# One of five convolution inputs is made by an accumulating DMA, and its siblings an iteration sooner

## The chip, the cores and the metric

The kernel runs on one core of a Trainium2 chip. The metric is the device time of one execution in microseconds; runs of one kernel lie within some tenths of a per cent of each other. A core has five engines that run side by side, each with its own queue of instructions: TensorE (PE in the profile, its weight loads PEld), VectorE (DVE), ScalarE (ACT), GpSimd (POOL) and SyncE (SP), which issues nearly all DMAs here. An instruction waits for semaphores of other engines at the head of its queue, and everything behind it in that queue waits too.

## The reference

Four modulated 1-D convolutions (64 channels, 3 taps, no activation between them) are run one after the other on each of 128 samples of 64 x 1024 floats, and the result is added to the input. Each sample has its own weights: the shared weight, scaled per input channel by a style vector and normalised per output channel.

```python
def _layer(x, style, w, b, mw, mb, typ):
    s = style @ mw.T + mb
    weight = SCALE * w * s[:, None, :, None]
    demod = lax.rsqrt(jnp.sum(weight * weight, axis=(2, 3)) + EPS)
    weight = weight * demod[:, :, None, None]
    if typ == 'same':         # layers 0 and 2
        out = conv_same(x, weight) + b
    elif typ == 'upsample':   # layer 1
        out = blur(conv_up(x, weight) + b, 2.0 * blur_k, (1, 1))
    elif typ == 'downsample': # layer 3
        out = conv_down(blur(x, blur_k, (2, 2)), weight) + b
    return out

out = x
for i, typ in enumerate(('same', 'upsample', 'same', 'downsample')):
    out = _layer(out, cond_512, weights[i], biases[i], mod_w[i], mod_b[i], typ)
return x + out
```

## The kernel before

**One convolution in place of four.** With nothing nonlinear between the layers, their chain is, away from the ends of a row, one convolution of nine taps whose weights differ from sample to sample. The kernel works out these nine taps for each sample on TensorE (stage1, stage2, stage3: small 64x64 matmuls), adds the residual as an identity in the middle tap, and applies them to the row. The ends of the rows are worked out apart, in a few extra slots of matmuls.

**Fewer products by sums and differences.** A row is stored as three planes (every third element), so that nine taps make three output planes out of three times three products. Instead of nine products per group, the kernel makes five: it forms five inputs T0 to T4 from sums and differences of the planes, five weight sets (three of them, H, by `combine_a` and `combine_b` on VectorE), multiplies them (`conv0` to `conv4`, each 24 records of 64x64 weights on 340 columns) and adds up the outputs (`sum1`, `sum2`, `output`).

**Tiling.** Four samples make a quad: two in the upper and two in the lower 64 partitions of two tiles, so that four 64x64 matmuls use the array at once. There are NQ = 32 quads. Each quad's input X holds 128 partitions x 2 x 3 planes of 344 floats (PL = 344).

**The inputs of a quad q.** X has two buffers, G one, each of T04, T12 and T3 two:

- `in_g2(q)` and `in_g01(q)` (VectorE, L768 and L763, both recorded at L712): G, three planes made out of X
- `in1(q)`: T1 = G plane 2 + G plane 1 (GpSimd, L776)
- `in2(q)`: T2 = G plane 2 - G plane 1 (GpSimd, L781)
- `in04(q)`: T0 and T4, differences of G's planes (VectorE, L790)
- `in3(q)`: T3 = a difference of X's planes (VectorE, L761)

**The order.** All instructions are written out by hand; no planner reorders them. The early turns (`early_turn`, quads 0 to 3) and the last three quads have orders of their own. The steady turn is `turn_of(q)`, for q = 4 to 28. With n = q+1, c = q+2 and s = q+4, a turn finishes quad q, does most of n, starts on the inputs and taps of c, and runs stage1 of s. On TensorE a steady turn is: stage2 of c (`stage2_rest`, L589 and L506), conv2(q), stage3_b(c), conv4(q), stage3_a(c), conv3(n), stage1_a(s), conv0(q), stage1_b(s), `share` (L506), an extra slot in turns 10, 14, 15 and 19 (L1044), conv1(n).

What the steps of the prediction touch, by engine:

- VectorE, in this order: sum2(q) (L712 into Y, then L862), combine_a(n) and combine_b(n) (L712 into H, L709), in04(n), share_sums (L501), in_g2(c), the side work of the turn (dictionary `SIDE`, work for the rows' ends and for constants, another one in each turn), stage1_b's sums (L481), in_g01(c), rest of an extra slot, sum1(n) (L712 into y), in3(c).
- GpSimd: r_sums(c) (L638, two of R's slots are sums), in2(n), now and then tables, stage1_b's addition (L484), in1(c).
- ScalarE: copies and scalings out of PSUM (L399), the outputs (L880), `share_copy` (L529). share_copy writes the PSUM banks that stage1_b's sums have read, and stage2_rest of the next quad adds onto what it wrote.
- SP: the loads of X (L146) and the stores of the outputs (L885).

Before a steady turn q starts, T1(n) has thus been made at the end of turn q-1, T2(n) follows in turn q behind R's sums, and T0/T4(n) in the middle of turn q on VectorE.

Of the kernel before, what the change touches and what calls it, by code (L numbers as in the profile page):

```python
# [48 lines left out]
F32 = mybir.dt.float32  # L49
AF = mybir.ActivationFunctionType  # L50
ALU = mybir.AluOpType
# [12 lines left out]
def kernel(  # L64
# [10 lines left out]
    NP, P, NXC = x.shape  # L75
    B = 2 * NP
    NQ = B // 4
# [5 lines left out]
    nc_v, nc_a, nc_g = nc.vector, nc.scalar, nc.gpsimd  # L83
# [3 lines left out]
    const = ctx.enter_context(tc.tile_pool(name="const", bufs=1))  # L87
# [4 lines left out]
    wf_pool = ctx.enter_context(tc.tile_pool(name="wf_pool", bufs=3))  # L92
    tpool = ctx.enter_context(tc.tile_pool(name="tpool", bufs=2))
    mpool = ctx.enter_context(tc.tile_pool(name="mpool", bufs=1))
    gpool = ctx.enter_context(tc.tile_pool(name="gpool", bufs=1))
    opool = ctx.enter_context(tc.tile_pool(name="opool", bufs=2))
    ps_conv = ctx.enter_context(tc.tile_pool(name="ps_conv", bufs=2, space=PSUM))
    ps_w = ctx.enter_context(tc.tile_pool(name="ps_w", bufs=1, space=PSUM))
# [39 lines left out]
    PL = NXC // 3  # L138
# [35 lines left out]
    NB = 340  # L174
# [222 lines left out]
    def scaled_copy(eng, dst, src, f):  # L397
        if eng is nc_a:
            nc_a.activation(dst, src, AF.Copy, scale=f)  # L399
        else:  # L400
            eng.tensor_scalar(dst, src, f, None, op0=ALU.mult)
# [158 lines left out]
    def stage2(q, pool=None, engs=(nc_a, nc_a), between=None):  # L560
        if q in shared_ps:
            ps = stage2_rest(q)
        else:
            ps = opened.pop(q, None)
            taps = range(9) if ps is None else range(3, 9)
            ps = stage2_taps(q, taps, ps or unit(pool or ps_w, f"psR{q}"))
        if between:
            between()
        t = r_pool.tile([P, 2, 9, C], F32, tag="R", name=f"R{q}")
        for r in range(2):  # L570
            scaled_copy(engs[r], flat(t[:, r, :7]), ps[r][:, : 7 * C], tC[:, q, r : r + 1])
        chain[q] = t
        return ps
# [3 lines left out]
    def stage2_taps(q, taps, ps):  # L577

        st = chain[q]
        for n in taps:  # L580
            e = n - 2
            if e % 2 == 0:
                a, lo, m = slice(1, 4), e // 2 + 1, 3
            else:
                a, lo, m = slice(4, 6), (e + 3) // 2, 2
            for r, rows in enumerate(HALF):
                for c, cols in enumerate(HALF):
                    src = st[c if r == 0 else 1 - c]
                    nc.tensor.matmul(  # L589
                        ps[r][cols, lo * C : (lo + m) * C],  # L590
                        E[rows, e + 2, :],
                        src[rows, a, :],
                        start=(n == 0),
                        stop=(n == 8),
                        skip_group_check=True,
                    )
        return ps
# [38 lines left out]
    def r_sums(q, eng):  # L636
        t = chain[q]
        eng.tensor_add(t[:, :, 7:9], t[:, :, 2:6:3], t[:, :, 3:7:3])  # L638
# [97 lines left out]
    Ts = {}  # L736
    Gs = {}
# [5 lines left out]
    def plane(buf, i, pairs=BOTH_PAIRS):  # L743

        at = PL * (2 - i) if i < 3 else PL * 2 + 1
        return buf[:, pairs, at : at + NJ]
# [16 lines left out]
    def in_g01(q, pairs=BOTH_PAIRS):  # L763
        if q < NQ:
            X, g = g_tile(q)
            sum_of(g[:, pairs, PL:], X[:, pairs, : 2 * PL], 0.5, X[:, pairs, PL:], ALU.subtract)

    def in_g2(q, pairs=BOTH_PAIRS):  # L768
        if q < NQ:
            X, g = g_tile(q)  # L770
            sum_of(plane(g, 2, pairs), plane(X, 3, pairs), 0.5, plane(X, 2, pairs), ALU.subtract)

    def in1(q, eng):
        if q < NQ:
            t, g = t_tile(q, "T12"), Gs[q]
            eng.tensor_add(t[:, :, 0, :NJ], plane(g, 2), plane(g, 1))  # L776

    def in2(q, eng):
        if q < NQ:
            t, g = t_tile(q, "T12"), Gs[q]  # L780
            eng.tensor_sub(t[:, :, 1, :NJ], plane(g, 2), plane(g, 1))  # L781

    def in04(q, pairs=BOTH_PAIRS):
        if q < NQ:
            t, g = t_tile(q, "T04"), Gs[q]
            a, b = g[:, pairs, :NJ], g[:, pairs, 2 * PL : 2 * PL + NJ]
            both = lambda v, step: bass.AP(
                v.tensor, v.offset, [*(list(d) for d in v.ap[:-1]), [step, 2], [1, NJ]]
            )
            nc_v.tensor_sub(t[:, pairs, :, :NJ], both(a, PL), both(b, 1))  # L790

    def product(q, m, ps, groups=range(K), alone=False):

        W, H_ = Wq[q]
        tag, i = SLOT[m]
        for g in groups:
            for s, rows in enumerate(HALF):
                for c, cols in enumerate(HALF):
                    if m in (0, 4):
                        w = W[rows, tap(m // 2, g), c, :]  # L800
                    else:
                        w = H_[rows, m - 1, g, c, :]
                    nc.tensor.matmul(  # L803
                        ps[s][cols, :NB],
                        w,
                        Ts[q, tag][rows, c, i, g : g + NB],
                        start=(g == 0 and (m == 3 or alone)),
                        stop=(g == K - 1),
                        skip_group_check=True,
                    )  # L810
# [36 lines left out]
    def sum1(q):  # L847

        y1w[q] = m_tile("y1", q, 2)
        for s, a in parts(q):  # L850
            sum_of(y1w[q][:, s], a, 2.0, m3c[q][:, s])
# [4 lines left out]
    def sum2(q, steps=(0, 1)):  # L856
        if 0 in steps:
            m3 = m3c.pop(q)
            for s, a in enumerate(banks(q)):
                sum_of(Y[:, s, :NB], m3[:, s], 3.0, a[:, :NB])  # L860
        for s, a in parts(q) if 1 in steps else ():
            nc_v.tensor_sub(y1w[q][:, s], y1w[q][:, s], a)  # L862
# [24 lines left out]
            os[q][:, s, planes].rearrange("c i j -> c (i j)"),  # L887
        )


    raw = const.tile([P, 512], F32, name="raw")

    WIDE = 6
    ends_ps = {}
# [94 lines left out]
    g1 = const.tile([P, 6, C], F32, name="g1")  # L989

    Ye = [const.tile([P, HB, 8], F32, name=f"Ye{s}") for s in range(2)]
    Ue = [const.tile([P, HB, 11], F32, name=f"Ue{s}") for s in range(2)]
    Ve = [const.tile([P, HB, 12], F32, name=f"Ve{s}") for s in range(2)]
    Oe = const.tile([P, B, 3], F32, name="Oe")
# [295 lines left out]
    def small(q):  # L1290
        l, bs = SMALL[q]
        dst = high(bs.stop - bs.start)
        src = c0f if l == 0 else cc[l - 1]
        for cols in HALF:
            nc.tensor.matmul(
                dst[cols], wsum[T, l, :], src[T, bs], start=False, stop=True, skip_group_check=True
            )
# [66 lines left out]
    def side(work, q):  # L1364
        work.get(q, lambda: None)()
# [117 lines left out]
    def turn_of(q):  # L1483
        n, c, s = q + 1, q + 2, q + 4
        entry = q == FIRST
        stage2(c)
        if entry:
            sum2(q)
            conv4(q)
            combine_a(n)  # L1490
            r_sums(c, nc_v)
        else:
            conv2(q)
            r_sums(c, nc_g)
            sum2(q)
            in2(n, nc_g)
        side(TABLES, q)
        for i in range(3):
            load(c + 1, slice(i, i + 1))
        stage3_b(c, open_a(n))  # L1500
        if entry:
            conv0(q, 0, 1)
        else:
            combine_a(n)
            conv4(q)
        stage3_a(c)
        combine_b(n)
        conv3(n)
        if entry:
            copy_m3(n)  # L1510
            stage1_a(s)
        outputs(q, 2)
        if not entry:
            if s < NQ:
                stage1_a(s)
            copy_m3(n)
        in04(n)
        if sharing(q):
            share_sums(c + 1)
        in_g2(c)  # L1520
        side(SIDE, q)
        if q in SMALL:
            l, bs = SMALL[q]
            nc_v.memset(high(bs.stop - bs.start), 0.0)
        conv0(q, *((2,) if entry else range(K)))
        if entry:
            conv1(n, 0, 1)
        outputs(q, 1)
        if s < NQ:
            stage1_b(s)  # L1530
        in_g01(c)
        if sharing(q):
            share(c + 1, banks(q))
            share_copy(c + 1)
        outputs(q, 0)
        if q in SLOTS:
            matmuls, width, rest = SLOTS[q]
            slot(matmuls, width, Y_banks)
            rest()
        if s == NQ:  # L1540
            slot(ends3, 3, unit(ps_w, "psE"), 3)
            rest3()
        conv1(n, *((2,) if entry else range(K)))
        if q in SMALL:
            small(q)
        sum1(n)
        in3(c)
        side(LATE, q)
        if s == NQ:
            in04(c)  # L1550
        in1(c, nc_g)
        if s + 1 < NQ:
            scale3(s + 1)

# [3 lines left out]
        turn_of(q)  # L1558

    q, n, c = NQ - 3, NQ - 2, NQ - 1  # L1560
    stage2(c)
    conv2(q)
    in2(n, nc_g)
    stage3(c, 0)
    sum2(q, (0,))
    combine_a(n)
# [26 lines left out]
    q, n = NQ - 2, NQ - 1  # L1593
# [128 lines left out]
```

## Time and profile before

| | |
|---|---|
| median of 3 runs | 475.84 us (475.61 to 476.85) |
| profiled execution, span | 475.5 us (first to last instruction; of this execution no other time is given) |
| TensorE busy / weight loads | 469.7 us / 349.5 us |
| VectorE, ScalarE, GpSimd busy | 417.3, 312.0 and 165.8 us |
| granted clock of TensorE | 0.998 |
| DMA | 70.71 MB, queue of SP 46.3% of 16 engines |

A line of the timeline reads: start, duration, engine, line, operation, output<-input with partitions x elements, count, and in brackets the idle time of the engine ahead of it with what ended it. Neighbouring instructions of one kind are merged (x2 and so on). Where a helper records many operations they all carry its line: L712 is `sum_of`, L399 `scaled_copy`. Lines of the page's fifth part give a group: its count, its busy time and the mean duration of one in ns. Matmuls overlap, so the pace of TensorE is read from the distance between starts.

### The profile page before, as it was taken

The page shows a single profiled execution, that of the slowest core. Times are in us where ns is not written, and L with a number is a line of the kernel's source. Part 1 is how long each engine was busy: PE and PEld are TensorE (multiplying, and loading weights), DVE is VectorE, ACT ScalarE, POOL GpSimd, SP SyncE. Part 2 cuts the span into 40 slices and gives each one's busy share as a digit, 9 for nine tenths or more (in the row PEclk, how much of TensorE's full clock was granted, in tenths as well). Part 3 has the DMA queues.
Part 4 walks back from the last instruction along what each step waited for, and adds up shares of the span by engine and source line. Part 5 has one row for each costly group of instructions (what it writes and reads, how often), then busy time and mean ns, then how long its engine had stood idle before and what let it go on. Part 6 is the DMA issues. An engine that isn't in the chain of part 4 may idle for free.

```text
span 475.5 us, 26771 instructions
## 1 busy us (share of the span) xinstructions
PE 469.7 (99%) x11932; PEld 349.5 (74%) x11932; DVE 417.3 (88%) x694; ACT 312.0 (66%) x711; POOL 165.8 (35%) x200
## 2 busy tenths in 40 slices
PE   9999999999999999999999999999999999999996
PEld 6987788777678876677776677766788787876653
DVE  3889998879989998899979899979998999999896
ACT  4565657577766676766667666667666777766464
POOL 3634033664444342233432233422333423243200
PEclk9999999999999999999999999999999999999999
DMA  5237456535445554345544454543555544455225
GB/s 176 71 115 224 150 151 180 152 113 177 139 145 166 166 166 136 123 150 169 163 150 126 130 168 152 178 124 121 152 164 169 164 145 147 148 152 161 80 91 193
DMA packets 52707, 70.71 MB, mean 149 GB/s; under 512 B 6000, under 2 KB 50672, under 8 KB 52592
## 3 DMA queue, kind: packets, MB, share of 16 engines
q1 hardware_dynamic: 52368, 68.78, 46.3%
q8 instruction: 93, 1.52, 1.4%
q10 hardware_dynamic: 224, 0.22, 0.1%
q14 instruction: 22, 0.18, 0.1%
HBM read 35.36 MB, written 33.62 MB: 145 GB/s over the span
## 4 chain that ended last, share of the span: by engine, by line
PE 99%; DVE 0%; ACT 0%; issue 0%
PE psA L803 47%; PE Y L803 12%; PE psR L506 9%; PE psW L621 7%; PE psA L621 7%; PE psS L428 6%; PE psR L589 5%; PE psA L506 2%; PE Y L1044 2%; PE Y L183 1%; PE Y L379 1%; PE psM L220 0%; PE psE L1044 0%; PE Y L255 0%; DVE o L882 0%; PE psM L255 0%
## 5 line engine op out<-in xcount | busy, mean ns | idle before, releaser
L803 PE MATMUL psA<-T,H 64*64 64x340 f32 x2304 | 185.9, 446 | 0.0
L803 PEld LDWEIGHTS psA<-T,H 64*64 64x64 f32 x2304 | 90.7, 133 | 46.9 <-issue 2.5
L712 DVE SCALAR_TENSOR_TENSOR G<-X 128x1376 f32<-128x1376 f32 (+2 forms) x65 | 78.0, 1206 | 0.2
L776 POOL TENSOR_TENSOR T<-G 128x684 f32<-128x684 f32 x28 | 46.3, 1652 | 73.7 <-DVE G L712 73.7
L484 POOL TENSOR_TENSOR S<-S 128x128 f32<-128x128 f32 x28 | 21.6, 772 | 139.7 <-ACT S L399 139.6
L399 ACT ACTIVATE R<-psR,tC 128x448 f32<-128x448 f32 x63 | 36.6, 631 | 43.6 <-PE psR L506 25.8
L803 PE MATMUL psA<-T,Wf 64*64 64x340 f32 x768 | 63.7, 446 | 0.0
L803 PE MATMUL Y<-T,Wf 64*64 64x340 f32 x768 | 62.4, 451 | 0.0
L712 DVE SCALAR_TENSOR_TENSOR Y<-m,psA 128x340 f32<-128x340 f32 x62 | 32.0, 516 | 28.2 <-PE psA L803 26.9
L399 ACT ACTIVATE psW<-psA 128x128 f32<-128x128 f32 x100 | 19.3, 268 | 49.1 <-PE psA L621 45.0
L790 DVE TENSOR_TENSOR T<-G 128x1368 f32<-128x1368 f32 (+1 forms) x33 | 50.8, 1541 | 0.0
L399 ACT ACTIVATE Wf<-psW,t 128x256 f32<-128x256 f32 (+2 forms) x76 | 32.7, 480 | 26.7 <-PE psW L621 26.4
L761 DVE TENSOR_TENSOR T<-X 128x684 f32<-128x684 f32 x32 | 47.7, 1492 | 0.0
L506 PE MATMUL psR<-S,E 64*64 64x64 f32 (+1 forms) x1472 | 46.8, 237 | 0.0
L781 POOL TENSOR_TENSOR T<-G 128x684 f32<-128x684 f32 x28 | 46.5, 1660 | 0.0
L428 PEld LDWEIGHTS psS<-wd,w2n 64*64 64x64 f32 x1120 | 35.1, 133 | 12.9 <-issue 0.3
L506 PEld LDWEIGHTS psR<-S,E 64*64 64x64 f32 x1472 | 39.5, 134 | 4.9 <-ACT psR L529 0.2
L803 PEld LDWEIGHTS Y<-T,Wf 64*64 64x64 f32 x768 | 30.3, 132 | 16.8
L803 PEld LDWEIGHTS psA<-T,Wf 64*64 64x64 f32 x768 | 29.8, 133 | 14.5
L880 ACT ACTIVATE o<-psA,tb,td 128x340 f32<-128x340 f32 x63 | 37.1, 648 | 5.0 <-PE psA L803 2.8
L880 ACT ACTIVATE o<-y,tb,td 128x340 f32<-128x340 f32 x62 | 38.5, 678 | 0.0
L880 ACT ACTIVATE o<-Y,tb,td 128x340 f32<-128x340 f32 x62 | 36.1, 639 | 2.8 <-PE Y L803 2.0
(180 smaller groups left out, 840.4 us busy)
## 6 DMA issues: line engine op xcount, KB each, us to landing
out<-o SPq DMA_DIRECT2D x191, 170.0 KB, 2.6
X<-in_x SPq DMA_DIRECT2D x150, 172.0 KB, 3.4
X<-in_x SPq DMA_DIRECT2D x14, 516.0 KB, 5.0
par<-in_params SPq DMA_DIRECT2D x3, 192.0 KB, 3.8
Xe<-in_x_ends SPq DMA_DIRECT2D x1, 512.0 KB, 4.5
out<-Oe SPq DMA_DIRECT2D x2, 96.0 KB, 2.1
out<-o ACTq DMA_DIRECT2D x1, 170.0 KB, 2.8
par<-in_params SPq DMA_DIRECT2D x1, 160.0 KB, 2.7
```

The source lines that it names most:

```text
L399: nc_a.activation(dst, src, AF.Copy, scale=f)
L428: nc.tensor.matmul(ps[r][cols, at * C : (at + n) * C], weight[rows], wd[c if r == 0 else 1 - c][rows, taps], start=first, stop=last, skip_ ...
L506: nc.tensor.matmul(dst[r][cols], weight[rows], st[c if r == 0 else 1 - c][rows, slots, :], start=False, stop=last, skip_group_check=True,)
L589: nc.tensor.matmul(ps[r][cols, lo * C : (lo + m) * C], E[rows, e + 2, :], src[rows, a, :], start=(n == 0), stop=(n == 8), skip_group_check ...
L621: nc.tensor.matmul(dst[r][cols], weight[rows], t[rows, c, slots, :], start=first, stop=last, skip_group_check=True,)
L712: nc_v.scalar_tensor_tensor(out, x, f, y, op0=ALU.mult, op1=op)
L761: nc_v.tensor_sub(t[:, pairs, 0, :NJ], plane(X, 3, pairs), plane(X, 1, pairs))
L776: eng.tensor_add(t[:, :, 0, :NJ], plane(g, 2), plane(g, 1))
L781: eng.tensor_sub(t[:, :, 1, :NJ], plane(g, 2), plane(g, 1))
L790: nc_v.tensor_sub(t[:, pairs, :, :NJ], both(a, PL), both(b, 1))
L803: nc.tensor.matmul(ps[s][cols, :NB], w, Ts[q, tag][rows, c, i, g : g + NB], start=(g == 0 and (m == 3 or alone)), stop=(g == K - 1), skip_ ...
L880: nc_a.activation(dst, src, AF.Identity, bias=add, scale=d3)
```

## The change

`in1_dma(q)` takes the place of `in1` for quads 6 to 30. It adds G's plane 1 onto G's plane 2 in place, by a DMA with `accum_op=add` that GpSimd issues, and `product` then reads T1 from G instead of T12. Since it overwrites plane 2, it comes after in2 and in04 of the same quad, and these move: in2(c) and in04(c) are made at the end of turn c-2 and no longer in turn c-1. In exchange in_g01(c) moves up, right behind in_g2(c). The DMA of n is issued in turn q behind r_sums(c), where in2(n) stood. G gets two buffers, and to make room `raw`, a scratch tile of the setup, becomes a view of Ye[0]. In the entry turn (q = 4) in04(n) stays where it was.

```diff
-    gpool = ctx.enter_context(tc.tile_pool(name="gpool", bufs=1))
+    gpool = ctx.enter_context(tc.tile_pool(name="gpool", bufs=2))
...
+    def in1_dma(q):
+
+        g = Gs[q]
+        nc_g.dma_start(plane(g, 2), plane(g, 1), accum_op=ALU.add)
+        first_of[q] = g[:, :, :PL]
+
+    first_of = {}
...
         tag, i = SLOT[m]
+        if m == 1 and q in first_of:
+            src = first_of[q]
+        else:
+            src = Ts[q, tag][:, :, i]
...
-                        Ts[q, tag][rows, c, i, g : g + NB],
+                        src[rows, c, g : g + NB],
...
-    raw = const.tile([P, 512], F32, name="raw")
...
+    raw = Ye[0].rearrange("c b e -> c (b e)")
...
             conv2(q)
             r_sums(c, nc_g)
+            in1_dma(n)
             sum2(q)
-            in2(n, nc_g)
...
-        in04(n)
+        if entry:
+            in04(n)
         if sharing(q):
             share_sums(c + 1)
         in_g2(c)
+        in_g01(c)
         side(SIDE, q)
...
         if s < NQ:
             stage1_b(s)
-        in_g01(c)
...
         if q in SMALL:
             small(q)
+        in2(c, nc_g)
         sum1(n)
         in3(c)
         side(LATE, q)
-        if s == NQ:
-            in04(c)
-        in1(c, nc_g)
+        in04(c)
...
     q, n, c = NQ - 3, NQ - 2, NQ - 1
+    in1_dma(n)
     stage2(c)
     conv2(q)
-    in2(n, nc_g)
     stage3(c, 0)
```

## The prediction

> **What bounds the kernel now.** I read the page's busy line first, then the chain that ended last, then TensorE's timeline, to see whether a busy TensorE is also one that is never held up.
>
> ```profile
> span 475.5 us, 26771 instructions
> PE 469.7 (99%) x11932; PEld 349.5 (74%) x11932; DVE 417.3 (88%) x694; ACT 312.0 (66%) x711; POOL 165.8 (35%) x200
> ...
> PE 99%; DVE 0%; ACT 0%; issue 0%
> ```
>
> TensorE is busy for 469.7 of 475.5 us and the chain that ended last is 99% TensorE: 5.8 us is all that it is idle. Busy does not say that it is at its limit, so I look at how far apart its steps start, in a middle turn and in the tail (columns: start, duration, engine, line, operation).
>
> ```profile
> 327.89 1.90 PE L803 MATMUL psA<-T,Wf 64*64 64x340 f32 x24
> 329.61 0.41 PE L428 MATMUL psS<-wd,w2n 64*64 64x64 f32 x16
> ...
> 465.62 1.92 PE L803 MATMUL psA<-T,H 64*64 64x340 f32 x24
> 467.33 1.92 PE L803 MATMUL Y<-T,Wf 64*64 64x340 f32 x24
> ```
>
> A convolution of 24 matmul records starts its successor 1.72 us later in the middle (327.89 to 329.61) and 1.71 us later in the tail, where GpSimd does nothing at all. The pace is the same in crowded and quiet places, so it is TensorE's own. A whole turn can be timed by sum2's first VectorE instruction:
>
> ```profile
> 291.57 1.07 DVE L712 SCALAR_TENSOR_TENSOR Y<-m,psA 128x340 f32<-128x340 f32 x2 [0.67 <-PE psA L803]
> 305.52 1.07 DVE L712 SCALAR_TENSOR_TENSOR Y<-m,psA 128x340 f32<-128x340 f32 x2 [0.39 <-PE psA L803]
> 321.97 1.07 DVE L712 SCALAR_TENSOR_TENSOR Y<-m,psA 128x340 f32<-128x340 f32 x2 [1.93 <-PE psA L803]
> 335.81 1.07 DVE L712 SCALAR_TENSOR_TENSOR Y<-m,psA 128x340 f32<-128x340 f32 x2 [0.84 <-PE psA L803]
> 349.65 1.07 DVE L712 SCALAR_TENSOR_TENSOR Y<-m,psA 128x340 f32<-128x340 f32 x2 [0.83 <-PE psA L803]
> ```
>
> 321.97 to 335.81 and 335.81 to 349.65 are 13.84 us each; 291.57 to 305.52 is 13.95. (305.52 to 321.97 holds an extra slot of matmuls.) In every one of these turns VectorE sat idle before sum2 until TensorE's conv2 had ended (0.39 to 1.93 us): TensorE sets the turn, VectorE waits for it. The change leaves every matmul in place. It can therefore win only stalls, and the slow turn shows 0.11 us of them. I put the most that it can gain at about 1 us in all, under 0.3% (1.4 us), which is about what a measurement of this kernel can tell from no change. So the question is what the moved work might delay.
>
> [...]
>
> **The change part by part.** In a steady turn q (n = q+1, c = q+2) GpSimd loses in1 and gains a DMA issue; in2(c) moves from after the next turn's r_sums to this turn, behind stage1_b's addition. VectorE's in04 goes from the middle of the turn to its end, and in_g01 moves up to where in04 stood. Here is turn 18, which rest1_edges (L1102) marks, first VectorE and GpSimd, then the two engines that follow:
>
> ```profile
> 296.45 1.58 DVE L790 TENSOR_TENSOR T<-G 128x1368 f32<-128x1368 f32 x1
> 298.27 0.87 DVE L712 SCALAR_TENSOR_TENSOR G<-X 128x684 f32<-128x684 f32 x1
> 299.06 1.39 DVE L1102 SCALAR_TENSOR_TENSOR Ue<-b1s,Ue 64x64 f32<-64x64 f32 x4
> 300.48 0.61 DVE L481 SCALAR_TENSOR_TENSOR S<-psS,tB,S 128x128 f32<-128x128 f32 x2
> 301.00 1.58 DVE L712 SCALAR_TENSOR_TENSOR G<-X 128x1376 f32<-128x1376 f32 x1
> 302.50 0.86 DVE L712 SCALAR_TENSOR_TENSOR y<-psA,m 128x680 f32<-128x680 f32 x1
> 303.28 1.86 DVE L761 TENSOR_TENSOR T<-X 128x684 f32<-128x684 f32 x1
> ...
> 298.63 0.82 POOL L484 TENSOR_TENSOR S<-S 128x128 f32<-128x128 f32 x1 [5.15 <-ACT S L399]
> 302.76 1.65 POOL L776 TENSOR_TENSOR T<-G 128x684 f32<-128x684 f32 x1 [3.30 <-DVE G L712]
> ...
> 300.92 0.63 ACT L529 COPY psR<-psA 128x256 f32<-128x256 f32 x2 [0.62 <-DVE S L481]
> ...
> 299.80 1.90 PE L803 MATMUL psA<-T,H 64*64 64x340 f32 x24
> 301.51 0.42 PE L506 MATMUL psR<-S,E 64*64 64x128 f32 x6
> ```
>
> *VectorE's order.* in04 (296.45) and in_g01 (301.00) take 1.58 us each. Exchanging them leaves the start of the side work (299.06) and of stage1_b's sums (300.48) where they are. At the end of the turn, sum1 can start when conv1 ends (299.80 + 1.90 = 301.70), and sum1 0.86, in3 0.86 (in3's 1.86 us here is a wait, next paragraph) and in04 1.58 end by 305.0; sum2 is not due before 305.52. Cost nothing, with 0.5 us to spare; if that cover went, conv4 behind sum2 would wait for each tenth over. In turn 20 the same count gives 335.4 against 335.81. TensorE needs T0 and T4 of c only in the next turn.
>
> *The shared access of VectorE and GpSimd.* in3 starts at 303.28 while GpSimd's in1 runs from 302.76 to 304.41, and takes 1.86 us; 304.41 plus 0.72 is when it ends. So a VectorE instruction that reads two SBUF operands stands still until GpSimd's two-operand instruction is through. The change takes in1 away and in3 becomes 1 us shorter. That gain lies in VectorE's idle time before sum2, so it is worth nothing to TensorE. But in2(c), with the same shape, now gets ready as soon as in_g01(c) has ended, at about 299.06, right when the side work and then the sums are next on VectorE. What is queued behind: stage1_b's sums (300.48), for those ScalarE's share_copy (300.92 to 301.55), for that TensorE's stage2_rest (301.51). In turn 18 this chain has no slack left.
>
> in2's price and the way the two engines take turns come from these rows:
>
> ```profile
> L781 POOL TENSOR_TENSOR T<-G 128x684 f32<-128x684 f32 x28 | 46.5, 1660 | 0.0
> ...
> 60.36 0.55 DVE L712 SCALAR_TENSOR_TENSOR H<-Wf 128x384 f32<-128x384 f32 x1
> 60.84 1.86 DVE L709 SCALAR_TENSOR_TENSOR Wf<-idn,t,Wf 128x64 f32<-128x64 f32 x2
> ...
> 60.46 1.96 POOL L781 TENSOR_TENSOR T<-G 128x684 f32<-128x684 f32 x1
> ```
>
> An in2 takes 1.66 us alone (1660 ns). At 60.46 one is queued directly behind an in1, VectorE's H at 60.36 is waiting, and in2 takes 1.96: H was let in between the two (0.55, not held up), and in2 paid the 0.3. Then VectorE's next instruction (60.84) took 1.86 for what else takes half a microsecond: it waited for all of in2. So they alternate. In the new turn: stage1_b's GpSimd addition (waiting since 298.63) goes at 299.06, one VectorE side instruction next, then in2 for 1.66 us, then the rest of the side work. A turn whose side work is one instruction loses nothing; one with several has its sums 1.66 us later. Two turns outside the extra slots have several two-operand side instructions: 18 (four) and 13 (two, L1016):
>
> ```profile
> 226.48 1.00 DVE L1016 SCALAR_TENSOR_TENSOR g<-par,g 128x192 f32<-128x192 f32 x2
> ...
> 227.84 0.63 ACT L529 COPY psR<-psA 128x256 f32<-128x256 f32 x2
> ...
> 228.94 0.40 PE L506 MATMUL psR<-S,E 64*64 64x128 f32 x8
> ```
>
> Turn 18: share_copy's last instruction ends at 301.55, level with stage2_rest's start at 301.51, so all of the 1.66 us comes through, a stall of 1.7. Turn 13: the copy ends at 228.47 + 1.66 = 230.13, due 228.94, a stall of 1.2. Sum 2.9 us. Turns 10 and 15 also have several, but extra matmuls ahead of conv1 as cover (turn 19, whose rows stand above, is 2.6 us longer through its slot). Turns 5 and 6 are uncertain:
>
> ```profile
> 113.74 0.26 DVE L981 SCALAR_TENSOR_TENSOR cc<-b1s,cc 128x96 f32<-128x96 f32 x1
> ...
> 112.97 0.88 POOL L484 TENSOR_TENSOR S<-S 128x128 f32<-128x128 f32 x1 [3.54 <-ACT S L399]
> ```
>
> There the two-operand side instruction reaches VectorE at 113.74, only 0.11 us before the addition ends (113.85). If in2 gets in first, each of these turns may lose up to 1 us; I take zero and keep 2 us for the range.
>
> *The DMA.* It is issued behind r_sums and conv1 waits for it. The trace of before has no such DMA; the nearest rows are SP's loads.
>
> ```profile
> X<-in_x SPq DMA_DIRECT2D x150, 172.0 KB, 3.4
> X<-in_x SPq DMA_DIRECT2D x14, 516.0 KB, 5.0
> ...
> 321.53 0.73 POOL L638 TENSOR_TENSOR R<-R 128x256 f32<-128x256 f32 x1 [3.92 <-ACT R L399]
> ...
> 330.19 1.90 PE L803 MATMUL psA<-T,H 64*64 64x340 f32 x24
> ```
>
> From r_sums' end (322.26) to conv1 (330.19) there are 7.9 us, and more in the four turns with an extra slot. 172 KB land in 3.4 us and 516 KB in 5.0: 1.6 us for 344 KB. The DMA adds 128 x 684 floats, 342 KB: by these rows 4.2 us if it moves its bytes once, 7.4 us if three times (two reads and a write). To that comes the issue on GpSimd, which no row shows: from nothing to one of its longest steps here, 1.7 us. Bounds 4.2 to 9.1 us; I take 6, between the two transfers, nearer the plain load, and so hidden: cost nothing. Below nothing is excluded, since TensorE waited nowhere for in1. GpSimd's queue behind it holds only an addition 6 us later. [...]
>
> *The rest.* A second G buffer takes G's reuse off the matmuls; raw's new place is read only before Ye is first written. SP's queue keeps its order, and the loads wait for in3, which ends earlier. The early turns and the tail's in1 and in2 of the last group stay.
>
> Sum: 475.5 + 2.9 = 478.4 by the profiled execution, whose span is all of its time that is given; the median of the runs, 475.84, is 0.34 above that span, so 478.7.
>
> **The rivals.**
>
> *Not slower: in2 gets no turn between.* The price appears only if in2 is served ahead of the second side instruction. If VectorE keeps its access over back-to-back instructions, in2 starts after the last of them, beside the sums, which read PSUM, and nothing is lost: 475.8. For it: side instructions follow each other without a gap. Against: the addition at 298.63 already gets in between in_g2 and the side work. Chance 25%.
>
> *in2 keeps the access.* If in2 follows the addition at once, every side instruction waits, in the 14 other turns with a single one as well:
>
> ```profile
> 329.45 0.94 DVE L1123 TENSOR_TENSOR Ve<-Ve,c 128x512 f32<-128x512 f32 x1
> ...
> 330.74 0.63 ACT L529 COPY psR<-psA 128x256 f32<-128x256 f32 x2
> ...
> 331.90 0.29 PE L506 MATMUL psR<-S,E 64*64 64x128 f32 x4
> ```
>
> There the copy ends at 331.37 and is due at 331.90, so 1.66 costs 1.1 us; 14 x 1.1 + 2.9 + 2 = 20 us, 496. Against it stands the 60.46 row. Chance 9%.
>
> *The DMA is late.* With 9.1 us against 7.9 conv1 waits 1.2 us in some 20 turns: 24 us, 500; it decides from 7.9 us on, and each further microsecond adds 20. Chance 18%.
>
> [...] Chance 4%.
>
> **How the numbers follow.** The forecast, 478.7, has 44%; its own range is 477 to 481 (one stall, or turns 5 and 6 as well). From 475.2 to 496.5 the range holds the forecast, the not-slower case and in2 keeping the access, 78%, plus a DMA that is late by a little or in a few turns; beyond it lie most of the late DMA and the gain. Faster by over 0.3% 4%; within 0.3% the 25% and 4% for a forecast with only one small stall, 29%; slower 67%.
>
> **What would show it.** Right: turns of 13.84 us everywhere but 13 and 18, there 15.0 and 15.6; in3 at 0.86 us in all of them; in2 on GpSimd some 0.5 us after in_g01, with the second side instruction of turn 18 starting or ending behind it; the DMA landing under 7.9 us; no wait of TensorE on a DMA. Wrong: a gap ahead of conv1 in each turn (late DMA), side instructions of over 2 us in turns 20 to 27 (in2 keeps the access), or no turn changed at all.

## The result, and the profile after

The changed kernel takes 480.12 us (median, 479.61 to 480.61) against 476.35 us (475.61 to 477.11) for the kernel before, of which one run was added to the three above: a ratio of 1.008, with a 95% interval of 1.0064 to 1.0096, so 3.8 us slower (3.0 to 4.6). A ratio here and below leaves out runs over 1.5% above the fastest of their kernel, which only the kernel with four DMAs has (three of six). The profiled execution took 480.31 us with a span of 478.5. Its page, busy line and chain:

```profile
span 478.5 us, 26777 instructions
PE 471.2 (98%) x11932; PEld 355.2 (74%) x11932; DVE 404.1 (84%) x694; ACT 312.4 (65%) x711; POOL 157.9 (33%) x200
...
PE 80%; issue 6%; POOL 5%; DMA 3%; DVE 3%; SPq 1%; ACT 1%; POOLq 0%; DVEq 0%; ACTq 0%
```

TensorE now idles for 7.3 us in place of 5.8. VectorE is busy for 404.1 us where it was 417.3, GpSimd for 157.9 where it was 165.8: both engines were relieved, and the time rose. The chain, 99% TensorE before, now leaves it at times for GpSimd, the DMA and VectorE. Where the microseconds are shows when turns are timed as in the prediction, by sum2's first instruction (VectorE's timeline):

```profile
293.19 1.07 DVE L712 SCALAR_TENSOR_TENSOR Y<-m,psA 128x340 f32<-128x340 f32 x2 [0.44 <-PE psA L815]
308.49 1.07 DVE L712 SCALAR_TENSOR_TENSOR Y<-m,psA 128x340 f32<-128x340 f32 x2 [1.39 <-PE psA L815]
325.18 1.07 DVE L712 SCALAR_TENSOR_TENSOR Y<-m,psA 128x340 f32<-128x340 f32 x2 [0.44 <-PE psA L815]
339.03 1.07 DVE L712 SCALAR_TENSOR_TENSOR Y<-m,psA 128x340 f32<-128x340 f32 x2 [0.44 <-PE psA L815]
352.87 1.07 DVE L712 SCALAR_TENSOR_TENSOR Y<-m,psA 128x340 f32<-128x340 f32 x2 [0.44 <-PE psA L815]
```

Turns 20 and 21 (325.18 to 339.03 to 352.87) are 13.85 and 13.84 us, as before. Turn 18 (293.19 to 308.49) is 15.30 us. All turns of which the length changed by 0.2 us or more, worked out in this way from both traces:

| turn | before | after | difference |
|---|---|---|---|
| 5 | 14.01 | 14.53 | +0.52 |
| 6 | 14.00 | 14.50 | +0.50 |
| 7 | 13.85 | 14.16 | +0.31 |
| 13 | 13.84 | 14.78 | +0.94 |
| 18 | 13.95 | 15.30 | +1.35 |
| 19 | 16.45 | 16.69 | +0.24 |
| 22 | 14.23 | 13.89 | -0.34 |
| 25 | 13.84 | 14.19 | +0.35 |

With the small remainders the turns 5 to 27 are 3.86 us longer. Turns 13 and 18 make 2.29 of it, turns 5 to 7 make 1.33. (The spans differ by 3.0 us only: up to turn 5 the trace of before took 0.7 us longer, and behind turn 27 it took 0.1 longer.) Turn 18 on the four engines, the view that the prediction argued from:

```profile
298.38 2.36 DVE L712 SCALAR_TENSOR_TENSOR G<-X 128x684 f32<-128x684 f32 x2
300.67 2.75 DVE L1113 SCALAR_TENSOR_TENSOR Ue<-b1s,Ue 64x64 f32<-64x64 f32 x4
303.45 0.61 DVE L481 SCALAR_TENSOR_TENSOR S<-psS,tB,S 128x128 f32<-128x128 f32 x2
...
300.26 0.80 POOL L484 TENSOR_TENSOR S<-S 128x128 f32<-128x128 f32 x1 [5.65 <-ACT S L399]
301.03 1.68 POOL L789 TENSOR_TENSOR T<-G 128x684 f32<-128x684 f32 x1
...
303.89 0.63 ACT L529 COPY psR<-psA 128x256 f32<-128x256 f32 x2 [1.98 <-DVE S L481]
...
301.60 1.89 PE L815 MATMUL psA<-G,H 64*64 64x340 f32 x22
304.30 0.60 PE L506 MATMUL psR<-S,E 64*64 64x128 f32 x6 [0.81 <-ACT psR L529]
```

GpSimd's addition runs from 300.26 to 301.06, in2 (L789) follows at 301.03, and the four side instructions (L1113), 1.39 us before, take 2.75. stage1_b's sums (L481) start at 303.45 behind them, share_copy follows, and TensorE, through with conv1, stands still until 304.30, by the bracket for ScalarE's copy. Turn 13, with its two side instructions, is the same picture:

```profile
227.15 2.35 DVE L1027 SCALAR_TENSOR_TENSOR g<-par,g 128x192 f32<-128x192 f32 x2
229.42 0.60 DVE L481 SCALAR_TENSOR_TENSOR S<-psS,tB,S 128x128 f32<-128x128 f32 x2
...
227.51 1.77 POOL L789 TENSOR_TENSOR T<-G 128x684 f32<-128x684 f32 x1
...
229.85 0.63 ACT L529 COPY psR<-psA 128x256 f32<-128x256 f32 x2 [1.45 <-PE psA L815]
...
230.26 0.60 PE L506 MATMUL psR<-S,E 64*64 64x128 f32 x6 [0.42 <-ACT psR L529]
```

A turn with one side instruction, turn 20:

```profile
332.66 0.95 DVE L1134 TENSOR_TENSOR Ve<-Ve,c 128x512 f32<-128x512 f32 x1
336.23 0.86 DVE L761 TENSOR_TENSOR T<-X 128x684 f32<-128x684 f32 x1
337.01 1.57 DVE L798 TENSOR_TENSOR T<-G 128x1368 f32<-128x1368 f32 x1
...
333.02 2.09 POOL L789 TENSOR_TENSOR T<-G 128x684 f32<-128x684 f32 x1
```

Here the side instruction keeps its 0.95 us and in2 pays, 2.09 us in place of 1.7. in3 takes 0.86, in04 ends at 338.58, and sum2 starts at 339.03 behind 0.44 us of waiting for TensorE. The turn is unchanged. And the DMA, from the DMA view, the groups by line, the tile's view and the waits:

```profile
G<-G POOLq DMA_DIRECT2D x25, 342.0 KB, 6.0
```
```profile
L781 POOL DMA_DIRECT2D G<-G x25 | 30.0, 1199 | 5.2 <-issue 5.2
```
```profile
DMA to landing us min/median/max: 4.3/6.0/8.6
```
```profile
PEld psR L506 <- ACT psR L529: 2.4, 2, 1.4
```

The last row is the stall of turns 13 and 18 as TensorE's weight loads see it: two waits for share_copy, 2.4 us in all. The DMA lands 6.0 us after its issue in the median, 4.3 at the least and 8.6 at the most, and the record of each issue on GpSimd is 1.2 us long. The longest landing is that of turn 5:

```profile
105.11 1.37 POOL L781 DMA_DIRECT2D G<-G  x1
...
113.88 1.95 PE L815 MATMUL psA<-G,H 64*64 64x340 f32 x24 [0.30 <-DMA G<-G]
```

105.11 + 8.6 is 113.7: conv1 would have started at about 113.4, and its bracket names the DMA. So the cover of turn 5 was 8.3 us, and that is most of its 0.52 us. Turn 6 has another kind of pause. TensorE's weight loads, and the DMA traffic of two stretches ahead of the pause's end:

```profile
125.77 0.78 PEld L815 LDWEIGHTS psA<-T,Wf 64*64 64x64 f32 x14
127.21 0.21 PEld L815 LDWEIGHTS psA<-T,Wf 64*64 64x64 f32 x8 [0.66 <-issue]
```
```profile
q8 instruction: 1, 0.02, 5.5%
```
```profile
q1 hardware_dynamic: 250, 0.32, 73.1%
```

"Issue" means that the profile shows nothing that TensorE waits for. In the stretch from 124.9 to 126.0 one packet of the queue that the profile calls instruction, by its name 16 KB of program code (all 93 packets of this queue are of 16 KB), went through the DMA engines (5.5% of 16 engines for 1.1 us is 0.97 us; in the trace from 124.96 to 125.92); from 126.0 to 127.2 there is none. The pause ends 1.29 us behind that packet. Turns 7 and 25 hold one such pause each (0.24 us at 135.3, 0.33 at 395.7), and the -0.34 of turn 22 is one that only the trace of before has (0.33 us at 350.9). The experiments come back to this.

### The profile page after: what moved, and what is told of

Same layout as the page of the kernel before. It is cut to its first block, busy times and chain, and to the rows that moved or that the text cites. A ratio compares the mean times of both kernels' runs of the same rounds, so it can differ in the third digit from the quotient of the medians.

```text
span 478.5 us, 26777 instructions
## 1 busy us (share of the span) xinstructions
PE 471.2 (98%) x11932; PEld 355.2 (74%) x11932; DVE 404.1 (84%) x694; ACT 312.4 (65%) x711; POOL 157.9 (33%) x200
## 4 chain that ended last, share of the span: by engine, by line
PE 80%; issue 6%; POOL 5%; DMA 3%; DVE 3%; SPq 1%; ACT 1%; POOLq 0%; DVEq 0%; ACTq 0%
PE psA L815 38%; PE Y L815 10%; PE psR L506 9%; PE psA L621 6%; PE psW L621 6%; PE psS L428 4%; PE psR L589 3%; DMA G<-G 2%; PE Y L1055 2%; DMA X<-in_x 2%; PE psA L506 1%; POOL T L789 1%; DVE G L712 1%; POOL T L776 1%; SPq L146 1%
## 5 line engine op out<-in xcount | busy, mean ns | idle before, releaser
L815 PE MATMUL psA<-T,H 64*64 64x340 f32 x1704 | 138.8, 446 | 0.0
L815 PEld LDWEIGHTS psA<-T,H 64*64 64x64 f32 x1704 | 69.5, 133 | 32.2 <-issue 1.7
L712 DVE SCALAR_TENSOR_TENSOR G<-X 128x1376 f32<-128x1376 f32 (+2 forms) x65 | 76.3, 1211 | 0.0
L484 POOL TENSOR_TENSOR S<-S 128x128 f32<-128x128 f32 x28 | 19.7, 703 | 150.1 <-ACT S L399 150.0
L789 POOL TENSOR_TENSOR T<-G 128x684 f32<-128x684 f32 x28 | 53.0, 1895 | 6.0 <-PE psA L815 6.0
L712 DVE SCALAR_TENSOR_TENSOR y<-psA,m 128x680 f32<-128x680 f32 x31 | 26.8, 865 | 30.2 <-PE psA L815 28.2
L638 POOL TENSOR_TENSOR R<-R 128x256 f32<-128x256 f32 x24 | 17.5, 728 | 97.5 <-DVE T L798 66.1
L506 PE MATMUL psR<-S,E 64*64 64x64 f32 (+1 forms) x1472 | 47.9, 238 | 1.2 <-ACT psR L529 1.2
L815 PE MATMUL psA<-G,H 64*64 64x340 f32 x600 | 48.1, 446 | 0.3 <-DMA G<-G 0.3
L506 PEld LDWEIGHTS psR<-S,E 64*64 64x64 f32 x1472 | 40.7, 134 | 6.7 <-ACT psR L529 2.4
```

Source lines behind the costliest of these rows:

```text
L484: nc_g.tensor_add(t[:, :, 2], t[:, :, 2], t[:, :, 0])
L506: nc.tensor.matmul(dst[r][cols], weight[rows], st[c if r == 0 else 1 - c][rows, slots, :], start=False, stop=last, skip_group_check=True,)
L712: nc_v.scalar_tensor_tensor(out, x, f, y, op0=ALU.mult, op1=op)
L815: nc.tensor.matmul(ps[s][cols, :NB], w, src[rows, c, g : g + NB], start=(g == 0 and (m == 3 or alone)), stop=(g == K - 1), skip_group_chec ...
```

## The experiments

The theory after this comparison: 2.3 us of the 3.8 come from in2's place among the side instructions of turns 13 and 18, and the rest, about 1 us, from the DMA, which the prediction had costed at nothing. The rival: the two long turns are a symptom of the DMA, and all of the loss goes with it.

**The order undone in two turns, the DMA kept** (`e1_sums_first`):

```diff
-        side(SIDE, q)
+        if q not in (13, 18):
+            side(SIDE, q)
...
             stage1_b(s)
+        if q in (13, 18):
+            side(SIDE, q)
```

> Kernel after, with the side work of turns 13 and 18 put behind stage1_b's sums instead of ahead of them. Theory (in2, now early, stands between the side instructions and holds up the sums of these two turns): turns 13 and 18 go back from 14.78 and 15.30 us to 13.84 to 13.95, the time falls by 2.3 us from 480.1 to about 477.8. Rival (the DMA and its traffic are the cost, the two turns are a side effect): the wait shows up elsewhere and the time stays at 480.

Measured: 477.08 us (474.63 to 479.29), ratio 1.0021 (1.0003 to 1.0039). Turn 18, VectorE's and TensorE's timelines:

```profile
299.07 0.61 DVE L481 SCALAR_TENSOR_TENSOR S<-psS,tB,S 128x128 f32<-128x128 f32 x2 [0.61 <-ACT o L892]
299.60 1.79 DVE L1113 SCALAR_TENSOR_TENSOR Ue<-b1s,Ue 64x64 f32<-64x64 f32 x4
...
299.13 1.90 PE L815 MATMUL psA<-G,H 64*64 64x340 f32 x24
300.85 0.40 PE L506 MATMUL psR<-S,E 64*64 64x128 f32 x8
```

The sums now come first, the side work waits for in2 behind them, and stage2_rest starts 1.72 us after conv1 with no wait. Turns 13 and 18 are 13.98 and 13.84 us. So the order's part is gone with the DMA still there, and about 1 us stays (0.1 to 1.9 by the interval).

**The order kept, the DMA taken out** (`e2_in_place_add`), by an addition of GpSimd at the same place, and **both** (`e3_both`), which is this with the edit above:

```diff
-        nc_g.dma_start(plane(g, 2), plane(g, 1), accum_op=ALU.add)
+        nc_g.tensor_add(plane(g, 2), plane(g, 2), plane(g, 1))
```

> Kernel after, with the accumulating DMA replaced by one addition of GpSimd in place (plane 2 += plane 1) at the same position; everything else as after. Theory: turns 13 and 18 stay at about 14.8 and 15.3 us, since in2 stands where it stood; turn 5 loses the 0.3 to 0.5 us of the first DMA; and the 1.8 us between span and time of after falls back to the 0.3 us of before, so about 478 us. Rival (the DMA is the whole cost): turns 13 and 18 are back at 13.84 and the time is that of before, 476.4. Second rival (the DMA costs nothing): 480.

Measured: 478.4 us (478.2 to 479.57), ratio 1.0053 (1.0035 to 1.0071), 2.5 us above before. Turns 13 and 18 are 14.80 and 15.33 us, turns 5 and 6 are back at 14.01 each, and the one wait of TensorE in the turns that is of any size is the same as in the changed kernel:

```profile
PE psR L506 <- ACT psR L529: 1.5, 2, 1.0
```

The expectation that the difference between time and span would fall was wrong: it is 1.8 us with and without the DMA.

> Both edits: sums ahead of the side work in turns 13 and 18, and GpSimd's addition in place of the DMA. Theory: all that was found is undone, the order of the inputs alone is left, 475.5 to 476.4 us, no measurable difference to before (476.4). Rival (something else in the moved order costs, such as in04 at the end of the turn): 477 or more.

Measured: 476.12 us (474.91 to 478.01), ratio 1.0001 (0.9987 to 1.0014); turns 13 and 18 are 13.97 and 13.84 us, turns 5 and 6 14.01. With both parts gone nothing is left that shows, within 0.7 us: the exchange of in04 and in_g01, the second G buffer and `raw`'s new place cost nothing, and the shorter in3 brings nothing. The parts add up: 2.5 us (order) and 1.0 (DMA) are 3.5, against 3.8 measured. The rival has fallen.

**Is it alternation?** If VectorE and GpSimd take turns, a turn with a single side instruction must lose as soon as that instruction is cut in two (`e5_side_in_two`, the single side instructions of turns 16, 17 and 20 to 27 done in two halves):

```diff
+    HALVES = slice(0, HB // 2), slice(HB // 2, HB)
+
+    def in_two(work):
+        def run():
+            for p in HALVES:
+                work(p)
+        return run
...
-        20: lambda: add2(0),
+        20: in_two(lambda p: add2_p(0, p)),
```

> Kernel after, with the single side instruction of turns 16, 17 and 20 to 27 written as two instructions of half the size, the same work. Theory (VectorE and GpSimd take turns, so the second instruction waits for all of in2): in these ten turns the sums come about 1.7 us later, against a slack of about 0.5, so each turn grows by 0.8 to 1.1 us and the time by 8 to 11, to 488 to 491. Rival (VectorE is not interrupted between back-to-back instructions, turns 13 and 18 have another cause): the ten turns stay at 13.84 to 13.9 and the time within 1 us of 480.

Measured: 489.94 us (one run). The ten turns are 14.85 to 14.98 us long, 1.0 to 1.14 over 13.84 each, while turns 13 and 18 stay at 14.78 and 15.30. Turn 20, and the waits of TensorE:

```profile
348.77 2.53 DVE L1362 TENSOR_TENSOR Ve<-Ve,c 128x256 f32<-128x256 f32 x2
351.20 0.58 DVE L481 SCALAR_TENSOR_TENSOR S<-psS,tB,S 128x128 f32<-128x128 f32 x2
...
349.13 1.85 POOL L789 TENSOR_TENSOR T<-G 128x684 f32<-128x684 f32 x1
```
```profile
PE psR L506 <- ACT psR L529: 6.5, 11, 1.0
```

The same elements in two instructions take 2.53 us instead of 0.95, since in2 runs between the halves; the wait that was there twice is there eleven times. The rival of the prediction by which VectorE keeps its access over back-to-back instructions has fallen, and so has the one by which a lone side instruction would wait too.

**What covers the transfer?** The DMA is issued behind stage1_b's addition, just ahead of conv1 (`e8_late_dma`):

```diff
             r_sums(c, nc_g)
-            in1_dma(n)
             sum2(q)
...
             stage1_b(s)
+        if not entry:
+            in1_dma(n)
```

> The changed kernel with the accumulating DMA issued behind stage1_b's addition instead of behind R's sums, so that it starts only some 0.5 us before conv1 wants the result. This shows what hides the transfer. Theory that the transfer takes 4.3 to 8.6 us and was covered by conv0 alone: each of some 24 turns is longer by about 5.5 to 6 us (landing 6.0 less the 0.5), so about 600 to 625 us, and the waits show TensorE at conv1 behind the DMA in each. Theory that the records put the landing later than the data is usable (the semaphore's share of it): the turn grows by less than the landing, 2 to 4 us each, 530 to 575 us.

Measured: 618.9 us (one run). The first theory had the time right, but not how it comes about. The groups by line, and TensorE in turn 19:

```profile
L815 PE MATMUL psA<-G,H 64*64 64x340 f32 x600 | 78.5, 676 | 96.0 <-DMA G<-G 85.6
```
```profile
325.61 3.47 PE L815 MATMUL psA<-G,H 64*64 64x340 f32 x24 [3.96 <-ACT wd L399]
```

TensorE idles for 96.0 us ahead of conv1, 4.2 us in each of 23 turns (turn 28 doesn't wait); the transfers land after 4.8 us in the median. Over the changed kernel each of the 23 turns costs 6.0 us. The other 1.9 us come after the wait: the records of conv1 take 676 ns on average instead of 446, one conv1 here 3.47 us instead of 1.90, and TensorE's granted clock is 0.58 and 0.50 in the first and the second half of this conv1, where it was 1.00 ahead of the wait (0.911 over the run, 0.999 in the changed kernel). In turn 10 the clock falls to 0.50 as well, behind a wait of 2.31 us. From what length of a wait on it falls, and why, no run shows. For the change itself the run says that the slots between R's sums and conv1 are what hides the transfer.

**What is the 1 us of the DMA?** Three more kernels build on `e1_sums_first`. The first has one small accumulating DMA early in the setup (`e7_early_dma`), for turn 5's late landing:

```diff
+    nc_g.dma_start(warm[:, 0], warm[:, 1], accum_op=ALU.add)
```

> As e1_sums_first, with one small accumulating DMA that GpSimd issues in the setup, long before the first turn. Theory that the first accumulating transfer of a launch lands late (8.6 us in the changed kernel, 7.5 in e1_sums_first, against a median of 6.0 and 5.8) because it is the first on its queue: the landing of turn 5's transfer falls to 5 to 6.5 us. Theory that landings scatter: it stays anywhere between 4.3 and 8.6, and so says little if it is low and speaks against the first theory if it is over 7. Time about 477 us in either case.

Measured: 477.13 us (one run), and turn 5's transfer lands after 7.6 us. It isn't late because it is the first on its queue. In the six other kernels with a DMA there it took 7.5, 7.9, 8.0, 8.3, 8.4 and 8.6 us, so turn 5 lies at the edge of its cover of 8.3; in `e1_sums_first`, with 7.5, the turn is 14.00 us, not longer than before. What makes that place slow is left open.

The second has another DMA of the same size in each turn, to a place that nothing reads (`e6_second_dma`):

```diff
         nc_g.dma_start(plane(g, 2), plane(g, 1), accum_op=ALU.add)
+        nc_g.dma_start(t_tile(q, "T12")[:, :, 0, :NJ], plane(g, 1))
```

> The changed kernel with the side work of turns 13 and 18 behind stage1_b's sums (as e1_sums_first) and with a second DMA per turn, of the same shape and size, that GpSimd issues right behind the accumulating one: it copies a plane of G into a part of T12's buffer that nothing reads. The part computed is unchanged. e1_sums_first stood at a ratio of 1.0021 to the kernel before, some 1.0 us above it. Theory that this 1.0 us is the price of the DMA traffic and of its issues, turn by turn: doubled traffic doubles it, to about 478.3 us (ratio 1.0042). Theory that it came from single landings near or beyond their budget (8.6 us in the first) and from gaps that vary between runs: the second transfer stands behind the first and holds nothing up, so the time stays within 0.4 us of e1_sums_first, about 477.1 (ratio 1.002). If the second transfer slows the landing of the first one beyond 7.9 us in many turns, each such turn is longer by the excess and TensorE's conv1 waits for it in the waits: up to 1 us a turn, 480 to 500 us.

Measured: 479.0 us (478.1 to 480.47), ratio 1.0068 (1.0048 to 1.0089). The accumulating DMA lands as before (5.8 us), nothing waits for the second one, and still the time rises by about 2 us over `e1_sums_first`, more than the doubling of the first theory gave (478.3). So it isn't a matter of landings. TensorE's waits:

```profile
PE psA L506 <- issue: 0.6, 1, 0.6
PE psR L589 <- issue: 0.5, 1, 0.5
PE psR L506 <- issue: 0.3, 1, 0.3
```

The third has four DMAs a turn, two of them to memory off the core (`e9_four_dmas`), beside `e1_sums_first` once more on the same chip (`e10_sums_first_again`):

```diff
+        nc_g.dma_start(sink[q % 2], plane(g, 1))
+        nc_g.dma_start(sink[2 + q % 2], plane(g, 1))
```

> The changed kernel with the side work of turns 13 and 18 behind stage1_b's sums and four GpSimd DMAs per turn: the accumulating one, the plain copy of e6_second_dma, and two more copies of the same plane to memory off the core. The part computed is unchanged. Of the runs so far, without the DMA and with the order undone the ratio was 1.0001, with one DMA 1.0021, with two 1.0068; in the traces TensorE's pauses put down to issue, of 0.3 to 0.75 us, ended 1.3 to 1.4 us after a packet of the instruction queue. Theory that traffic on the DMA engines costs, because packets with program code come later through it: the ratio rises further with four, to 1.011 to 1.02 (481 to 485.5 us), spread over turns in pauses of up to 1.5 us, each ending 1.3 to 1.4 us behind such a packet, with the accumulating DMA still landing under 7.9 us. Theory that GpSimd's issues cost (four of 1.2 us, its addition behind them): pauses would show TensorE waiting for ScalarE's or GpSimd's work at the same place of each turn. Theory that the rise from one DMA to two was scatter: the ratio stays at 1.002 to 1.007.

> e1_sums_first once more, beside e9_four_dmas on the same chip: the changed kernel with the side work of turns 13 and 18 behind the sums, one DMA per turn. By the first run of it 1.0021 to the kernel before (1.0003 to 1.0039). Theory that one DMA costs about 1 us: again 1.001 to 1.004. Theory that one DMA costs nothing: 0.9995 to 1.001.

Measured: four DMAs 506.48 us (499.49 to 511.49), ratio 1.0558 (1.0516 to 1.06; 1.063 by the median of all six runs); one DMA 476.9 us (475.88 to 479.32), ratio 1.0025 (1.0007 to 1.0044). The numbers expected for four were far too low, but the traces show the first theory's mechanism. TensorE's waits with four DMAs, then its weight loads in turn 6 and the DMA traffic ahead of the pause's end, from 125.2 to 126.3:

```profile
PE psR L506 <- issue: 8.6, 10, 1.7
PE psA L621 <- issue: 4.1, 9, 0.9
PE psA L819 <- issue: 1.5, 3, 0.8
PE psA L819 <- DMA G<-G: 1.1, 1, 1.1
```
```profile
127.75 0.21 PEld L819 LDWEIGHTS psA<-T,Wf 64*64 64x64 f32 x8 [1.44 <-issue]
```
```profile
q0 software_dynamic: 107, 0.33, 97.9%
q8 instruction: 1, 0.02, 5.3%
```

Of TensorE's waits in the turns only one, of 1.1 us, is for something named; 14.2 us are "issue", spread over many turns. A wait for ScalarE's or GpSimd's work at one place of each turn, which the second theory asked for, isn't there.

I compared the end of each such pause of the weight loads, of 0.29 us or more in turns 5 to 28 and outside the extra slots, with the packets of the instruction queue in the trace. The page counts 93 of them in the span, one in 5 us, so chance would put two or three of the 37 pauses below into the window of the table's third column. (`e8_late_dma`, in which TensorE waits for the DMA in each turn, is left out.)

| kernels | pauses | of them ending 1.25 to 1.61 us behind a packet | their sum by kernel |
|---|---|---|---|
| no such DMA (before, `e2`, `e3`) | 3 | 3 | 0.33, 0.36, 0.31 us |
| one (after, `e1`, `e5`, `e7`, `e10`) | 8 | 7 | 0.99, 0.91, 0.72, 0.87, 0 us |
| two (`e6`) | 2 | 2 | 1.23 us |
| four (`e9`) | 24 | 19 | 19.9 us |

The place of the pauses in the program says it more strictly. Count TensorE's records in the order of the program: two for a weight load and its matmul, one for a register or branch instruction. Then 35 of the 37 pauses stand ahead of a record whose number leaves 193 or 194 when it is divided by 256, in every kernel; among them are three of `e9_four_dmas` (1.84, 1.55 and 1.27 us) that end 2.3 to 2.7 us behind a packet. One packet comes for 258 of TensorE's records (93 for 23995 before). At these places, 72 in turns 5 to 28, TensorE goes on at the earliest 1.2 us behind a packet's end, in all ten kernels; at other places, 128 records ahead, it comes as near as 0.2 us and less. So I read these pauses as TensorE waiting for its program: 35 of 37 by their place, 31 by the packet ahead of them; the profile itself names no cause. Of the other two, one is a wait for a DMA that lands after 8.9 us (`e5`), and one of 0.45 us (`e9`) stays open.

With four DMAs there are many more of these pauses, and longer ones: 19.9 us, where turns 5 to 27 are 24.3 us longer than before. With none, one and two the pauses are few, but the times point the same way (ratios 1.0001, 1.0021 and 1.0025, 1.0068, 1.0558 with none, one, two and four). The packets themselves don't take longer (median in these turns 1.17 us before, 1.11 with four); they start later, in the median 1.08 us behind the last such place before and 1.79 us with four. What makes them start later, their queue or the engines, wasn't tried, nor whether the amount of the traffic or its way off the core does it. With a single DMA the rows show on average 0.4 us more of it than without, so that a part of the 1 us has no row.

## Why the prediction was right, and where it was not

- **TensorE sets the turn.** Right: 13.84 us in all turns without a stall, before and after, although VectorE is busy for 13 us less. What was taken off VectorE and GpSimd bought nothing (`e3_both`, 1.0001).
- **in2 among the side instructions of turns 13 and 18.** The step that carries the forecast is right in place and mechanism: both turns, and of the ordinary ones only these. Its size was too large, 2.9 us against 2.29 in the traces (1.35 for 1.7, 0.94 for 1.2) and 2.5 us by `e2_in_place_add`. The mis-sized term is the 1.66 us by which share_copy was to move. In turn 18 it ended 9.98 us behind the turn's sum2 before (301.55 - 291.57) and ends 11.33 behind it now (304.52 - 293.19); in turn 13 it went from 9.47 to 10.81. That is 1.35 and 1.34 us. An in2 that gets in between two side instructions takes the access for 1.68 to 1.77 us, but costs VectorE only 1.35, the same as the side work's own growth (1.39 to 2.75, 1.00 to 2.35).
- **Turns 5 and 6.** Zero was taken and 2 us kept for the range. They lost 1.0 us, but not by the race that was named: in turn 5 in2 and the side work got along, and conv1 waited for the DMA; in turn 6 TensorE stood still for 0.66 us behind a packet of the instruction queue.
- **The DMA.** The estimate of 6 us is the median that was measured, and the bounds of 4.2 to 9.1 hold all of 4.3 to 8.6. Its issue, bounded by 0 and 1.7 us, is 1.2. What failed is the conclusion "hidden: cost nothing". The transfer was hidden in all turns but turn 5, where 8.6 is over the cover of 8.3 us, and the DMA still cost about 1 us. The step looked only at who waits for the transfer, not at what else the 16 DMA engines carry: the instruction queue's 93 packets, 1.4% of them in the changed kernel. With four DMAs a turn GpSimd's queue has 97.9% of the 16 engines in the stretch ahead of turn 6's pause of 1.44 us, and the one instruction packet there 5.3%.
- **The exchange of in04 and in_g01.** Right: 0.44 us is left ahead of sum2 in turn 20 where the count gave 0.4.
- **The sum.** 2.9 us were forecast, 3.8 measured. The order was put 0.4 us too high (2.9 for 2.5), the DMA 1.0 us too low; the 0.3 us that remain lie within the interval (3.0 to 4.6). 480.12 is 1.4 us over the forecast of 478.7, since the kernel before, too, was 0.5 us longer in the comparison (476.35 for 475.84). The 0.34 us that the prediction added compares a time with a span; a span of 475.5 is a time of about 477.3 (last section). It changes nothing in 478.7, which is the median, 475.84, and 2.9.
- **The rivals.** "Not slower" fell by the L1113 row (2.75 us) and `e5_side_in_two`, "in2 keeps the access" by turns 20 to 27 at their old length, "the DMA is late" by the landings; it can be had by placing the DMA elsewhere, at a price of 6.0 us a turn (`e8_late_dma`). For the 4% of a gain no run shows a ground: turns without a stall stay at 13.84 us, and `e3_both` equals the kernel before.

## What to carry to other kernels

TensorE set the pace here and relieving the others bought nothing (1.0001 in `e3_both`), so each moved step has to be checked for what it now stands in front of: GpSimd's in2 got in at the next gap between two of VectorE's instructions, which cost nothing in turn 20 with its single side instruction (13.85 us for 13.84), and most of in2's length in turn 18 with four (1.35 of 1.7 us) and in the ten turns of `e5_side_in_two` with two (1.0 to 1.14 us). A DMA that lands in time is not free on that account (about 1 us here): look at the "issue" pauses of the busiest engine and at the instruction queue in the DMA view before and after traffic is added. And price a displaced wait by how much later the follower ends, not by the length of what it waits for.

## What the hardware showed that was not expected

- The instruction queue in the DMA view has 93 packets of 16 KB, 1.4% of the 16 engines, one for 258 of TensorE's records. TensorE's pauses without a named cause stand at the same place in every 256 records (35 of 37) and mostly end 1.25 to 1.61 us behind a packet (31 of 37); with four added transfers a turn they grow to 1.8 us (weight loads).
- The accumulating DMA of 342 KB within SBUF lands after 4.3 to 8.6 us in the changed kernel, 6.0 in the median; GpSimd's record of the issue is 1.2 us long, but the next issue starts 0.6 to 0.8 us after it has begun (`e6_second_dma`, `e9_four_dmas`).
- In turn 19 of `e8_late_dma` conv1 runs at about half its pace behind a wait of 3.96 us (3.47 us instead of 1.90, granted clock 0.58 and 0.50); over the run's 23 turns 1.9 us come on top of a wait of 4.2 each, nearly half as much again.
- Time less span is 1.7 to 1.9 us in all runs here, with GpSimd's DMA and without. The trace of before, with a span of 475.5, is then one of its longer executions, about 1 us over its median.
